# Layer 2 of a two-layer graph transformer: gathers two chunks ahead, four chunks of raw rows, ten of thirteen blocks of normalised rows turned inside rounds 0 and 1

## The chip, the core and the metric

The kernel runs on one core of one Trainium2 chip. The time is device microseconds of one execution, with all inputs and the output in the chip's memory; lower is better. Three runs of the kernel before gave 2701.38, 2709.74 and 2716.52 us, so the median is 2709.74 us.

The core has five engines, each with an instruction queue of its own that runs in order: TensorE (PE; PEld is its weight load), VectorE (DVE), ScalarE (ACT), GpSimd (POOL) and SyncE (SP). In this kernel SP issues most plain transfers, ACT issues a few, and POOL issues only the gathers of rows by index. Engines wait for each other, and for transfers, on semaphores.

## The reference

6250 nodes with 128 features and 106250 directed edges, sorted by target node. Two graph attention layers of 2 heads with 64 channels each; a batch norm and a ReLU between them; at the end a residual and a layer norm.

```python
def _transformer_conv(h, edge_attr, src, dst, Wq, bq, Wk, bk, Wv, bv, We, Ws, bs):
    q = (h @ Wq + bq).reshape(n, H, C)
    k = (h @ Wk + bk).reshape(n, H, C)
    v = (h @ Wv + bv).reshape(n, H, C)
    e = (edge_attr @ We).reshape(-1, H, C)
    alpha = jnp.einsum('ehc,ehc->eh', q[dst], k[src] + e) / jnp.sqrt(jnp.asarray(C, h.dtype))
    ex = jnp.exp(alpha - segment_max(alpha, dst)[dst])
    a = ex / segment_sum(ex, dst)[dst]
    out = segment_sum((v[src] + e) * a[:, :, None], dst)
    return out.reshape(n, H * C) + h @ Ws + bs

edge_attr = jnp.concatenate([cos((node_vec[src] - edge_weight) * time_w + time_b), msg], axis=-1)
h = _transformer_conv(x, edge_attr, ...layer 1)
h = relu((h - h.mean(0)) / jnp.sqrt(h.var(0) + 1e-05) * bn_g + bn_b)
x = _layernorm(x + _transformer_conv(h, edge_attr, ...layer 2))
```

## The kernel before

**Tiling.** The sorted edges are cut into NC = 106 chunks. A chunk has CE = 1024 edge slots (T = 8 tiles of 128) and NN = 64 target nodes, so 64 nodes times 2 heads fill the 128 partitions. All data is float32. The function `conv(c, extra, first_blocks)` (from L699) is called once for each layer, with c = 0 and c = 1. Everything is issued in an order written out by hand (`tc.manual_schedule()`), so the order of the Python calls is the order of each engine's queue.

**A round.** The loop at L934 has one round for each k. In round k of layer 2 PE does, in this order: `score(k, 0)` (L822 and L823: scores of 512 slots against the 128 node-and-head columns), `turn_weights(k-1)` (L845: 8 transposes of the exponentials), `score(k, 1)`, `finish_turn(k-2)` (L875, L876), `turn_in(k+1, 0)` and `turn_in(k+1, 1)` (L801: 4 transposes each of the gathered rows, tiles 0 to 3 and 4 to 7), some side work that `pull` takes from a generator (L627 and L1082: the score tables and the residual for later nodes), `finish(k-2)` (L897, L898), and `gather_sums(k-1)` (L853: 8 products that sum the rows by target node). DVE takes the lowest score (L828), divides by the softmax sum (L860 to L863, of k-2), copies the turned sums `fat` (L878, which L897 waits for) and copies the stored time encoding into the chunk (L982). ACT copies turned rows (L805, or L803 with batch norm and ReLU), turned weights (L846), and takes the exponential (L835).

**What a chunk needs from memory.** `fetch(k)` lets SP issue five loads in layer 2: the edge features (L726, 256 KB), the score table (L737, 128 KB), the time encoding `fz` (L740, 128 KB), the turned edge features `et` (L742, 448 KB) and the residual (L744, 32 KB). `gather(k, rows)` (L749) lets POOL fetch the 128 source rows of each of the 8 tiles, 64 KB each. Fetch and gathers run AHEAD = 4 chunks before use. From the second on, a gather in round k is tied to a step of PE in that round (`behind`): row 1 to `score(k, 0)`, row 2 to `turn_weights(k-1)`, row 3 to `score(k, 1)`, rows 4 and 5 to the two halves of `turn_in(k+1)`, and rows 6 and 7 to the second and the sixth product of `gather_sums(k-1)`.

**Buffers.** The chunk tile `ff` has AHEAD + 2 = 6 buffers, `fz` has 4, the residual 7, `et` 6. So in round k the tile of chunk k+4 takes the buffer of chunk k-2, whose last reader is `gather_sums(k-2)` in round k-1; and `fz` of chunk k+4 takes the buffer of `fz` of chunk k, which L982 reads late in round k. SP's queue stands at L740 until then.

**Between the layers.** Layer 1 leaves its result turned in SBUF (`hT`), and its rows unnormalised in memory (`h_d`). The batch norm's scale and shift are known once the last rows are there. Then `relu` (L1096) normalises `hT` block by block (13 blocks of 512 nodes), and `first_blocks` (L1098), called in the first round of layer 2, turns all 13 blocks back into rows and stores them to `hn_d`: for each block 4 transposes on PE (L1017), a copy on DVE (L1019, tile `fhr`, 3 buffers), and a store on SP (L1027, L1032). Chunks 0 to RAW - 1 = 2 do not wait for that: they gather raw rows from `h_d`, apply scale, shift and ReLU in the copy of the turned rows (L803), and normalise the rows themselves on DVE before they are summed (`normalise`, L868 and L869). From chunk 3 on rows come from `hn_d`; in the before kernel these gathers stand in round -1.

**Stores.** From round 11 of layer 2 on each round stores the output of one finished chunk: ACT scales it (`fout`, L923) and SP issues the store (L925), after SP's loads of that round.

Of the kernel before, what the change touches and what calls it, by code (L numbers as in the profile page):

```python
# [7 lines left out]
F32 = mybir.dt.float32  # L8
# [5 lines left out]
P = 128  # L14
D = 128
# [7 lines left out]
GE = GT * P  # L23
# [598 lines left out]
def tables(nc, pl, c, fT, b0, work, bank):  # L622

    o = work.tile([P, GE, H, 3 - c], F32, name="fo", tag="fo", bufs=1)
    for i, (a, b) in enumerate(pl.mats[c]):
        pg = bank()
        nc.tensor.matmul(pg, a, fT, start=True, stop=True)  # L627
        if i == 2 * H:
            nc.scalar.activation(o[:, :, :, 2], pg[:, :, None].to_broadcast([P, GE, H]), AF.Identity, bias=b)
        elif i < H:  # L630
            nc.scalar.activation(o[:, :, i, 0], pg, AF.Identity, bias=b)
        else:
            nc.vector.scalar_tensor_tensor(
                o[:, :, i - H, 1].rearrange("p (b n) -> p b n", n=P), pg.rearrange("p (b n) -> p b n", n=P), b,
                pl.code[:, None, :].to_broadcast([P, GE // P, P]), op0=OP.add, op1=OP.add)
# [25 lines left out]
def ordered(ctx: ExitStack, tc: tile.TileContext, pl, x, dst, edge_attr_64, conv2, bn_g, bn_b, out):  # L661
# [32 lines left out]

    SINGLE = 40

    RAW = 3

    def conv(c, extra, first_blocks=None):  # L699


        cs = ExitStack()
        load = cs.enter_context(tc.tile_pool(name=f"fload{c}", bufs=AHEAD + 2))
        work = cs.enter_context(tc.tile_pool(name=f"fwork{c}", bufs=2))
        small = cs.enter_context(tc.tile_pool(name=f"fsmall{c}", bufs=3))
        lnp = cs.enter_context(tc.tile_pool(name="fln", bufs=2)) if c else None
# [13 lines left out]
        def fetch(k):  # L720
            s = ch[k] = Plan()
            lo, hi = first(k)
            s.nb = nc.sync.value_load(pl.nbs[0:1, k:k + 1], min_val=lo, max_val=hi)
            sl = nc.sync.value_load(pl.sls[0:1, k:k + 1], min_val=0, max_val=E - CE)
            s.f = f = load.tile([P, T, FW], F32, name="ff")
            nc.sync.dma_start(f[:, :, 1 + D + TD:D + EW],  # L726
                              edge_attr_64[bass.ds(sl, CE), :].rearrange("(t p) d -> p t d", p=P))
            if c:
                nc.vector.memset(f[:, :, D + EW:1 + D + EW], 1.0)
            else:  # L730
                bits = small.tile([P, T, BITS], I32, name="fbits")
                nc.vector.tensor_tensor(bits, pl.dsts[:, :, k:k + 1].to_broadcast([P, T, BITS]),
                                        pl.bitm[:, None, :].to_broadcast([P, T, BITS]), OP.bitwise_and)
                nc.vector.tensor_scalar(f[:, :, D + EW:D + EW + BITS], bits, 0.0, None, op0=OP.is_equal)
                nc.vector.tensor_copy(f[:, :, D + EW + BITS:], bits)
            s.tab = load.tile([P, NN * H, 3 - c], F32, name="ftab")
            nc.sync.dma_start(s.tab, pl.tab_d[c][:, bass.ds(s.nb, NN)].rearrange("p n h w -> p (n h) w"))  # L737
            if c:
                s.z = load.tile([P, T, TD], F32, name="fz", bufs=AHEAD)
                nc.sync.dma_start(s.z, enc_d[k].rearrange("p (t d) -> p t d", d=TD))  # L740
                s.et = ets[k % len(ets)]
                nc.sync.dma_start(s.et, et_d[k])  # L742
                s.r = load.tile([NN, D], F32, name="fr", bufs=AHEAD + 3)
                nc.sync.dma_start(s.r, res_d[bass.ds(s.nb, NN), :])  # L744

        def gather(k, rows, behind=None):
# [7 lines left out]
                    behind = None  # L754

        shape = [P, T, TD]

        args, turned = [], []

# [56 lines left out]
        def score(k, u):  # L816

            s = ch[k]
            if u == 0:
                s.ps = p_s.tile([P, CE], F32, name="fps")  # L820
            w = slice(u * GE, (u + 1) * GE)
            nc.tensor.matmul(s.ps[:, w], s.tab[:, :, 0], s.ft[:, w], start=True, stop=False)  # L822
            return nc.tensor.matmul(s.ps[:, w], s.tab[:EC, :, 1], s.et[:, w], start=False, stop=True)  # L823
# [107 lines left out]
                next(gen, None)  # L931

        with cs, tc.manual_schedule():
            for k in range(-AHEAD, NC + 3):  # L934
                def on(j):
                    return 0 <= j < NC

                if on(k + AHEAD):
                    fetch(k + AHEAD)
                    gather(k + AHEAD, range(1))  # L940
                if k == -AHEAD and c:
                    first_blocks()
# [17 lines left out]
                if on(k + AHEAD):  # L960
                    gather(k + AHEAD, (4,), step)
                if on(k):
                    weigh(k)
                step = turn_in(k + 1, 1) if on(k + 1) else None
                if on(k + AHEAD):
                    gather(k + AHEAD, (5,), step)
# [12 lines left out]
                if c and on(k):  # L979
                    if k < RAW:  # L980
                        normalise(k)
                    nc.vector.tensor_copy(ch[k].f[:, :, 1 + D:1 + D + TD], ch[k].z)  # L982
# [3 lines left out]
                if on(k + AHEAD):  # L986
                    for t, step in zip((6, 7), steps):
                        gather(k + AHEAD, (t,), step)
# [9 lines left out]
    with tc.tile_pool(name="fpw", bufs=2) as pw:  # L998
# [3 lines left out]
        def pass_rows(b0):  # L1002

            r0 = b0 * GE
            n = min(GE, N - r0)
            rows = turned_rows(b0)
            nc.vector.bn_stats(stats[:, b0], hT[:, r0:r0 + n])
            yield
            put_rows(h_d, b0, rows)
            yield  # L1010

        def turned_rows(b0):
            r0 = b0 * GE
            n = -(-min(GE, N - r0) // P)
            pt = pl.bank().rearrange("p (b d) -> p b d", d=P)
            for i in range(n):
                nc.tensor.transpose(pt[:, i], hT[:, r0 + i * P:r0 + (i + 1) * P], ident)  # L1017
            rows = pw.tile([P, GE // P, P], F32, name="fhr", bufs=3)
            nc.vector.tensor_copy(rows[:, :n], pt[:, :n])  # L1019
            return rows  # L1020

        def put_rows(to, b0, rows):
            r0 = b0 * GE
            n = min(GE, N - r0)
            full = n // P
            if full:
                nc.sync.dma_start(to[r0:r0 + full * P, :].rearrange("(b p) d -> p b d", p=P), rows[:, :full])  # L1027

            left = n - full * P
            for a, b in ((0, left // 16 * 16), (left // 16 * 16, left)):  # L1030
                if a < b:
                    nc.sync.dma_start(to[r0 + full * P + a:r0 + full * P + b, :], rows[a:b, full])  # L1032

        def rest():
            def second():
# [304 lines left out]
```

## Time and profile before

| what | us |
|---|---|
| median of the three runs | 2709.74 |
| the profiled execution: its own time | 2705.18 |
| its span, first to last instruction | 2703.3 |
| granted TensorE clock, mean over the span | 0.947 |
| PE busy | 2331.9 |
| POOL busy (its gathers from `xv_d` 819.0, from `hn_d` 781.5) | 1628.4 |
| DVE busy / ACT busy | 1238.1 / 1234.0 |
| first `relu` block, after layer 1 has ended | 1371.62 |
| first gather of layer 2 | 1372.52 |
| first `turn_in` of layer 2 (chunk 0) | 1412.58 |
| start of round 3 of layer 2 | 1461.51 |
| last gather | 2645.20 |

The profile is of one execution. "Busy" is time in which an engine executes; the idle time of an engine that nobody waits for costs nothing. The chain of waits follows the work that ended last back from instruction to instruction, and tells at each step what released it. "Issue" is time in which an engine waited for nothing that the profile shows, and "remote", or "another core or an unknown queue", is a release whose sender the profile can't name. The times in a list of instructions are from the span's start.

### The profile page before, as it was taken

Reading aid. Unit: us, or ns where it says so; the run is one execution under the profiler, and the core shown is the slowest. Engines: PE = TensorE matmul, PEld = TensorE weight load, DVE = VectorE, ACT = ScalarE, POOL = GpSimd, SP = SyncE. Lnnn points to the kernel's source line nnn. Section 1 sums busy time; section 2 is a strip of 40 time slices with the busy share of each in tenths; the row PEclk is TensorE's granted clock in tenths of the full one; section 3 lists DMA queues with packets and bytes.
Section 4 is the critical chain, followed back from the end, with each engine's and each line's share of the span. In section 5 each row is a group of like instructions: output and inputs, shape, how many; then the busy total and the mean of one; then the engine's idle time right before and its main releaser. Section 6 shows DMA issues by size and latency. Waiting matters only on the chain. (4 is left out here: it accounts for less than half of the span.)

```text
span 2703.3 us, 40520 instructions
## 1 busy us (share of the span) xinstructions
PE 2331.9 (86%) x11586; PEld 1763.4 (65%) x11586; DVE 1238.1 (46%) x3738; ACT 1234.0 (46%) x1955; POOL 1628.4 (60%) x1717
## 2 busy tenths in 40 slices
PE   5799889998898998898957888898888889888887
PEld 3577667777776776776735666666666666666665
DVE  4466556666565665666533333333333333333223
ACT  2566666665555554545523333343333333333344
POOL 4666666666666666666336666666666666666660
PEclk7899999999999999999978999999999989999999
DMA  6555555555555455555447555565555555545441
GB/s 207 140 160 153 142 150 160 152 131 157 154 158 160 127 164 164 139 149 147 112 117 189 161 143 151 143 159 153 153 154 143 152 150 152 153 134 139 130 130 37
DMA packets 431127, 396.68 MB, mean 147 GB/s; under 512 B 279697, under 2 KB 375182, under 8 KB 427566
## 3 DMA queue, kind: packets, MB, share of 16 engines
q1 hardware_dynamic: 357680, 239.73, 31.9%
q0 software_dynamic: 54656, 113.07, 17.4%
q10 hardware_dynamic: 18558, 41.20, 4.3%
q8 instruction: 95, 1.56, 0.2%
q14 instruction: 138, 1.13, 0.1%
HBM read 277.19 MB, written 113.17 MB: 144 GB/s over the span
## 5 line engine op out<-in xcount | busy, mean ns | idle before, releaser
L749 POOL DMA_INDIRECT ff<-xv_d,fsrcs x848 | 819.0, 966 | 489.4 <-issue 169.6
L749 POOL DMA_INDIRECT ff<-hn_d,fsrcs x824 | 781.5, 948 | 462.4 <-issue 173.8
L853 PE MATMUL fpa<-ff,fpt 128*128 128x225 f32 x3392 | 754.2, 378 | 3.3 <-issue 2.7
L853 PEld LDWEIGHTS fpa<-ff,fpt 128*128 128x128 f32 x3392 | 675.9, 205 | 29.0 <-issue 6.2
L805 ACT COPY fft<-fpx 128x512 f32<-128x512 f32 x418 | 244.5, 585 | 579.2 <-PE fpa L853 164.6
L822 PE MATMUL fps<-fft,ftab 128*128 128x512 f32 x848 | 451.5, 614 | 45.4 <-ACT fs L835 24.4
L846 ACT COPY fpt<-fppt 128x512 f32<-128x512 f32 x424 | 234.7, 587 | 511.2 <-PE fppt L845 172.7
L878 DVE COPY fat<-fpo 128x256 f32<-128x256 f32 x212 | 90.0, 425 | 641.9 <-PE fpx L801 180.9
L845 PEld LDWEIGHTS fppt<-fident,fs 128*128 128x128 f32 x1696 | 199.5, 141 | 110.7 <-issue 106.7
L828 DVE TENSOR_REDUCE flow<-fps 128x1 f32<-128x1024 f32 x212 | 257.5, 1215 | 16.2 <-PE fpg L627 10.8
L835 ACT ACTIVATE fs<-fps,fm 128x1024 f32<-128x1024 f32 x212 | 236.8, 1117 | 34.0 <-DVE fm L830 14.6
L801 PE MATMUL fpx<-fident,ff 128*128 128x128 f32 x1696 | 240.5, 275 | 8.5 <-issue 7.2
L823 PE MATMUL fps<-fet,ftab 112*128 112x512 f32 x424 | 219.0, 597 | 8.7 <-issue 8.7
L845 PE MATMUL fppt<-fident,fs 128*128 128x128 f32 x1696 | 222.4, 273 | 3.5 <-issue 1.7
L823 PE MATMUL fps<-fxT,ftab 112*128 112x512 f32 x424 | 220.0, 600 | 2.8 <-issue 2.8
L822 PEld LDWEIGHTS fps<-fft,ftab 128*128 128x128 f32 x848 | 165.0, 227 | 64.9 <-ACT fs L835 37.1
L801 PEld LDWEIGHTS fpx<-fident,ff 128*128 128x128 f32 x1696 | 196.3, 142 | 15.3 <-issue 13.2
L823 PEld LDWEIGHTS fps<-fet,ftab 112*128 112x128 f32 x424 | 106.4, 251 | 85.7 <-issue 80.1
L897 PE MATMUL fpo<-fwv,fat 128*64 128x64 f32 x424 | 64.5, 246 | 110.7 <-issue 104.9
L811 ACT COPY fet<-fpe 112x512 f32<-112x512 f32 x212 | 126.5, 597 | 73.1 <-PE fpa L853 35.3
L823 PEld LDWEIGHTS fps<-fxT,ftab 112*128 112x128 f32 x424 | 84.4, 200 | 103.7 <-issue 103.0
L897 PEld LDWEIGHTS fpo<-fwv,fat 128*64 128x64 f32 x424 | 44.2, 146 | 158.9 <-issue 143.1
(202 smaller groups left out, 2438.1 us busy)
## 6 DMA issues: line engine op xcount, KB each, us to landing
ff<-in_edge_attr SPq DMA_DIRECT2D x212, 256.0 KB
et_d<-fet SPq DMA_DIRECT2D x106, 448.0 KB
fxT<-et_d SPq DMA_DIRECT2D x106, 448.0 KB
ftab<-tab_d SPq DMA_DIRECT2D x106, 192.0 KB
tab_d<-fo ACTq DMA_DIRECT2D x13, 1536.0 KB
ff<-xv_d,fsrcs POOLq DMA_INDIRECT x848
enc_d<-fzs SPq DMA_DIRECT2D x106, 128.0 KB
ftab<-tab_d SPq DMA_DIRECT2D x106, 128.0 KB
```

Source lines behind the costliest of these rows:

```text
L749: row = nc.gpsimd.indirect_dma_start(out=f[:, t, (1 if c else 0):1 + D], out_offset=None, in_=(h_d if k < RAW else hn_d) if c else pl.xv_d ...
L801: last = nc.tensor.transpose(px[:, t * P:(t + 1) * P], s.f[:, u * 4 + t, 1:1 + D], ident)
L805: nc.scalar.copy(s.ft[:, u * GE:(u + 1) * GE], px)
L811: nc.scalar.copy(s.et[:, u * GE:(u + 1) * GE], pe[:EC])
L822: nc.tensor.matmul(s.ps[:, w], s.tab[:, :, 0], s.ft[:, w], start=True, stop=False)
L823: return nc.tensor.matmul(s.ps[:, w], s.tab[:EC, :, 1], s.et[:, w], start=False, stop=True)
L828: nc.vector.tensor_reduce(low, s.ps, AX.X, OP.min)
L835: nc.scalar.activation(s.s, s.ps, AF.Exp, bias=s.bias, scale=-1.0)
L845: last = nc.tensor.transpose(pp[:, t * P:(t + 1) * P], s.s[:, at:at + P], ident)
L846: nc.scalar.copy(s.pt[:, u * GE:(u + 1) * GE], pp)
L853: nc.tensor.matmul(s.pa, s.pt[:, t * P:(t + 1) * P], s.f[:, t, 1:1 + D + EW], start=t == 0, stop=t == T - 1)
L897: nc.tensor.matmul(po[:NN, 0, r], at[:, 0, :, h], wv[c][:, r], start=True, stop=False)
```

## The change

Layer 1 keeps its order. In layer 2:

- `lead(k)` is 2: the loop starts at k = -2, and in round k the loads and gathers of chunk k+2 are issued instead of those of chunk k+4. The ties of each gather to a step of PE stay as they are. `ff`, the tables and `et` have 5 or 6 buffers (5 for the pool, `et` 6), `fz` 4, the residual 6.
- In the first round the first five gathers of chunk 0 are issued at once, and the other three are tied to the last product of the first table block (`pl.step`).
- `first_blocks` now only does the 12 remaining `relu` blocks. The 13 blocks of normalised rows are turned by `hide(n)`: one after each of the first three PE steps of round -1, five in round 0 and five in round 1, where they take the place of the `pull` of side work. The copies go to a tile of their own (`fhn`, 4 buffers). The first block of side work is so pulled from round 2 on.
- RAW is 4: chunk 3 gathers raw rows as well, and chunk 4, in round 2, is the first that reads `hn_d`.
- The flag `filling` is always False.

```diff
@@ tables @@
-        nc.tensor.matmul(pg, a, fT, start=True, stop=True)
+        pl.step = nc.tensor.matmul(pg, a, fT, start=True, stop=True)
...
-    RAW = 3
+    RAW = 4
+
+    hidden = list(range(-(-N // GE)))
...
-        load = cs.enter_context(tc.tile_pool(name=f"fload{c}", bufs=AHEAD + 2))
+        load = cs.enter_context(tc.tile_pool(name=f"fload{c}", bufs=5 if c else AHEAD + 2))
...
-                s.r = load.tile([NN, D], F32, name="fr", bufs=AHEAD + 3)
+                s.r = load.tile([NN, D], F32, name="fr", bufs=6)
...
+        def lead(k):
+            return 2 if c else AHEAD
+
+        def yield_first(bring):
+            if not c:
+                bring(range(T))
+                return
+            bring(range(5))
+            bring(range(5, T), pl.step)
+            first_blocks()
+
+        def hide(n):
+            step = None
+            for b0 in hidden[:n]:
+                step = put_rows(hn_d, b0, *turned_rows(b0, small.tile([P, GE // P, P], F32, name="fhn", bufs=4)))
+            del hidden[:n]
+            return step
...
-            for k in range(-AHEAD, NC + 3):
+            for k in range(-lead(-NC), NC + 3):
                 def on(j):
                     return 0 <= j < NC
 
-                if on(k + AHEAD):
-                    fetch(k + AHEAD)
-                    gather(k + AHEAD, range(1))
-                if k == -AHEAD and c:
-                    first_blocks()
-                step = score(k, 0) if on(k) else None
-                if on(k + AHEAD):
-                    gather(k + AHEAD, (1,), step)
-                step = turn_weights(k - 1) if on(k - 1) else None
-                if on(k + AHEAD):
-                    gather(k + AHEAD, (2,), step)
+                coming = [j for j in range(k + lead(k - 1), k + lead(k) + 1) if on(j)]
+                filling = False
+
+                def bring(rows, behind=None):
+                    for j in coming:
+                        gather(j, rows, behind)
+
+                for j in coming:
+                    fetch(j)
+                if k == -lead(-NC):
+                    yield_first(bring)
+                elif k < -1:
+                    bring(range(T))
+                elif not filling:
+                    bring(range(1))
+                step = score(k, 0) if on(k) else hide(1) if c and k == -1 else None
+                if k >= -1 and not filling:
+                    bring((1,), step)
+                step = turn_weights(k - 1) if on(k - 1) else hide(1) if c and k == -1 else None
+                if k >= -1 and not filling:
+                    bring((2,), step)
                 place()
                 if on(k - 2):
                     divide(k - 2)
-                step = score(k, 1) if on(k) else None
-                if on(k + AHEAD):
-                    gather(k + AHEAD, (3,), step)
+                step = score(k, 1) if on(k) else hide(1) if c and k == -1 else None
+                if k >= -1 and not filling:
+                    bring((3,), step)
...
                 if k >= 0:
                     at_round[0] = k
-                    pull(extra, 2 if k < 4 or k > 96 else 1)
+                    if c and k < 2:
+                        hide(5)
+                    else:
+                        pull(extra, 2 if k < 4 or k > 96 else 1)
...
@@ turned_rows, put_rows: return the last transpose; rows may be given @@
...
@@ first_blocks @@
             for b0 in range(1, NT):
                 relu(b0)
-            for b0 in range(-(-N // GE)):
-                put_rows(hn_d, b0, turned_rows(b0))
```

More of the change, by code (lines that the diff above doesn't have):

```diff
@@ L959, in conv @@
                 step = turn_in(k + 1, 0) if on(k + 1) else None
-                if on(k + AHEAD):
-                    gather(k + AHEAD, (4,), step)
+                if k >= -1:
+                    bring(range(5) if filling else (4,), step)
                 if on(k):
@@ L964, in conv @@
                 step = turn_in(k + 1, 1) if on(k + 1) else None
-                if on(k + AHEAD):
-                    gather(k + AHEAD, (5,), step)
+                if k >= -1:
+                    bring((5,), step)
                 for j in (k + 2,) if k < SINGLE else (k + 2, k + 3) if k == SINGLE else (k + 3,):
@@ L985, in conv @@
                 steps = gather_sums(k - 1) if on(k - 1) else (None, None)
-                if on(k + AHEAD):
+                if k >= -1:
                     for t, step in zip((6, 7), steps):
-                        gather(k + AHEAD, (t,), step)
+                        bring((t,), step)
             at_round[0] = 2 * NC
@@ L1008, in pass_rows, with turned_rows @@
             yield
-            put_rows(h_d, b0, rows)
+            put_rows(h_d, b0, *rows)
             yield
-        def turned_rows(b0):
+        def turned_rows(b0, rows=None):
             r0 = b0 * GE
@@ L1016, in turned_rows, with put_rows @@
             for i in range(n):
-                nc.tensor.transpose(pt[:, i], hT[:, r0 + i * P:r0 + (i + 1) * P], ident)
-            rows = pw.tile([P, GE // P, P], F32, name="fhr", bufs=3)
+                step = nc.tensor.transpose(pt[:, i], hT[:, r0 + i * P:r0 + (i + 1) * P], ident)
+            if rows is None:
+                rows = pw.tile([P, GE // P, P], F32, name="fhr", bufs=3)
             nc.vector.tensor_copy(rows[:, :n], pt[:, :n])
-            return rows
-        def put_rows(to, b0, rows):
+            return rows, step
+        def put_rows(to, b0, rows, step):
             r0 = b0 * GE
@@ L1032, in put_rows @@
                     nc.sync.dma_start(to[r0 + full * P + a:r0 + full * P + b, :], rows[a:b, full])
+            return step
         def rest():
```

## The prediction

> **What bounds the kernel now.** I read first the page's totals and slices, then the chain of waits between the layers, then the lists of instructions there, and last the rounds of layer 2.
>
> ```profile
> span 2703.3 us, 40520 instructions
> PE 2331.9 (86%) x11586; PEld 1763.4 (65%) x11586; DVE 1238.1 (46%) x3738; ACT 1234.0 (46%) x1955; POOL 1628.4 (60%) x1717
> ...
> PE   5799889998898998898957888898888889888887
> ...
> PEclk7899999999999999999978999999999989999999
> ```
>
> PE sets the time nearly everywhere, but slices 21 and 22 (1352 to 1487 us) fall to 5 and 7 tenths, with the granted clock down too: the passage between the layers. The chain of waits there:
>
> ```profile
> 1381.83 0.43 DVE fspread L1117
> 1382.25 3.56 another core or an unknown queue
> 1385.94 5.50 another core or an unknown queue
> 1391.53 6.21 another core or an unknown queue
> 1397.83 7.61 another core or an unknown queue
> ...
> 1422.17 5.39 issue
> ...
> 1431.08 11.77 another core or an unknown queue
> ```
>
> The columns are start, length, and what the chain stood on. The first line is work, the others are waits. The four after it are DVE's copies of the normalised rows (L1019): PE had turned those blocks by 1384.3, yet the copies start at 1385.89, 1391.46, 1397.76 and 1405.46. They make 22.9 us of signals that come late; the last two, 17.2 us, fall in rounds 0 to 2. While they last POOL issues gathers one after the other:
>
> ```profile
> 1401.29 0.95 POOL L749 DMA_INDIRECT ff<-h_d,fsrcs  x1 [0.30 <-issue]
> 1417.77 0.94 POOL L749 DMA_INDIRECT ff<-hn_d,fsrcs  x1 [15.53 <-DMA hn_d<-fhr]
> ```
>
> POOL has done its 24 raw gathers, then stands 15.5 us until `hn_d` is stored; chunk 0 could have been scored long before, but the 13 blocks stand ahead of it in PE's queue.
>
> Rounds, from the starts of L822 after L853: rounds 4 to 99 or so (94 that start between 1480 and 2600 us) take 11.94 us on average, though a round with no wait takes 10.15 (9.3 without side work). The difference is mostly L897, which waits for the copy `fat`. What SP does in that time:
>
> ```profile
> SPq L740 <- DVE ff L982: 105.3, 24, 9.0
> SPq L740 <- DVE finv L860: 84.5, 11, 10.2
> SPq L740 <- DVE finv L861: 58.3, 9, 8.8
> ```
>
> 248 us in which SP's queue stands at the load of `fz` (name of the wait, total, count, longest). The 448 KB load of `et` (L742) comes just behind it. Its place in the round goes with the round's length: where it is issued 3 to 1 us ahead of a round the round takes 10.22 us on average (20 rounds), at 1.5 to 3.5 us into it 12.72 (31 rounds), at 5 to 7 us 14.83 (3). In the first 5 us after it PE's signal to `fat` comes some 2 us late, after 6 us hardly late.
>
> **The change, part by part.**
>
> *The passage.* Before: 89.9 us from the first `relu` (1371.62) to the start of round 3 (1461.51). After: chunk 0's gathers still start at 1372.5 and take 8 x 1.25 us, to 1382.5; the `relu` blocks still end at 1384.2, and the table that chunk 0 needs is still stored at 1379.53 and loaded at 1384.30, with `fz`, `et` and the residual behind it. The three blocks turned in round -1 (12 transposes, about 2 us) lie beside that. Those loads kept the transfers busy until about 1391, so I let round 0 start at 1391 instead of 1414.1. Rounds 0 to 2 took 47.4 us. In them four L627 (0.95 us each at full clock) leave, 3.8 us, and ten blocks come in: 40 transposes, 0.66 to 1.1 us for four, 6.6 to 11 us; I take 10.8, since the clock is half there. DVE's ten copies (0.69 us each) and SP's stores lie beside other work. A copy waits for the store four before it to land; behind it in DVE's queue stand `normalise` of the same round and the next round's division, and `gather_sums` waits for `normalise`, one round later. The new tie of chunk 0's gathers 5 to 7 to the last table product (PE is done with it at 1378.18) costs nothing: POOL gets to the sixth at 1378.78. Of the 17.2 us of late signals I let 4 go, about a quarter, since most gathers of chunks 1 to 3 are now tied to a step of PE and run less in one stretch. Round 3 then starts at 1391 + 47.4 - 3.8 + 10.8 - 4 = 1441.4: a gain of 20 us. Bounds: if all of the 17.2 goes, 37; if the 22.9 us of late signals come back on ACT's copies of chunk 0, a loss of 3. The stores of `hn_d` (3.2 MB) now run against the loads of chunks 1 to 3; chunk 4's gather in round 2 needs them landed, and the last four took 2.4 us from issue to the gather's release, so nothing waits if round 1 issues them.
>
> *Fourth raw chunk.* `normalise` is 2 x 1.224 + 0.693 us of DVE (3.1 us) in round 3, between `fres` and the next division, where DVE has over 4 us until L875 is due; the ReLU copy costs 0.78 instead of 0.59 us on ACT. Nothing on the path; if that cover were gone, 3 us. The gathers that overlapped the three L868 pairs took 1.26, 1.31 and 1.35 us instead of 0.95, the next ones 0.98: 0.4 us of POOL. [...]
>
> *Two ahead instead of four.* A gather of row 7 tied to `gather_sums` in round k must have landed at the second half of `turn_in` in round k+1, and no longer two rounds later. POOL lags: in the trace row 7 starts 2.6 us (median) before that point. From issue to the last packet of a gather I see 2.7 us (the one at 1401.29, no packet after 1404) to 4 us (the last one, 2645.20, packets until 2649). At 3.3 us, 57 of 94 rounds would stand, 70 us in all, but in the same rounds PE stands afterwards anyway for L897; what goes beyond that is 20 us at 3.3, 38 at 4.0, 92 at 5.0. PE's standing also lets POOL catch up, and row 0 no longer waits for `gather_sums`, which alone cuts the 20 to 5. I take 10, between these two. The Trainium skill (DMA: Bandwidth & Descriptors, Anatomy of one DMA) has about 2.0 us plus bytes over 436 GB/s: an estimate of 2.15 us for 64 KB, with POOL's 0.95 us 3.1 us; by it the sum would be some 5 us lower.
>
> *SP's queue.* `fz` of chunk k+2 takes the buffer of k-2, so the wait of 248 us goes; so do POOL's and SP's waits for `gather_sums(k-2)` at row 0 and L726. SP then stands at the output store instead (L925, behind `fout`), and the five loads go out together, about 1 MB. From `fout` to the store are 0.42 us, from there to L726 2.3 to 4.3, to `et` 1.6 more: `et` first comes about 3 us into the next round, the long kind; but lateness there delays `fout`, and so the next `et`, towards 5 to 8 us. Late rounds: (20 x 10.22 + 3 x 14.83) / 23 = 10.82; early: 12.72. With half of each 11.77, that is 0.17 us less than now, over some 92 rounds 16 us. Bounds: all early, 92 x 0.78 = +72; all late, 92 x 1.12 = -103.
>
> *The end.* Gathers go on for two more rounds (to round 103). Rounds after the last gather take 9.3 us, those with gathers 11.94: +5.3.
>
> *Sum.* 2705.2 (the profiled execution) - 20 + 0 + 10 - 16 + 5.3 = 2684.5. The median of the runs shown stands 4.6 above that execution; I add half of it: **2687 us**.
>
> **The rivals.** (1) *SP's burst locks early* (slower): the 1 MB leaves 1 to 3 us into every round and each `fat` is late. For it: the 31 rounds at 12.72; against: each late round pushes the next burst later. 2687 + 16 + 72 = 2775; it decides once over about a fifth more of the rounds than half are of the early kind. (2) *Row 7 becomes the wait* (slower): if a gather lands 5 us after issue, +92 - 10: 2769; it decides above about 4.3 us. For it: POOL's lag; against: 2.7 to 4 us seen. (3) *The burst locks late*: rounds of 10.82, 2687 + 16 - 103 = 2600. (4) *The passage gives nothing*: the ten blocks keep their late signals inside rounds 0 and 1, and the change only moves the stall: 2687 + 20 = 2707.
>
> **How the numbers follow.** Forecast (2650 to 2696) 0.36; (3) and values below 2650 0.17; (4) 0.13; (1) 0.19; (2) 0.15. A measurement of this kernel can tell about 0.5% (13.5 us), so faster is below 2696: 0.53; same 0.13; slower (above 2723) 0.34. Range 2600 to 2778 leaves out some 0.1 at each side; the likeliest case alone spans 2650 to 2696.
>
> **What would show it.** Right: the first `turn_in` of layer 2 near 1385 and round 3 near 1441; POOL's 15.5 us gap gone; no wait of L740 on L982; L801's second half waiting for gathers under 0.3 us a round; mean round of 11.4 to 11.8. Wrong: L801 waiting for `ff` by 1 us or more in most rounds (2); L897 at 7.5 us or later in nearly all rounds with L742 at 1.5 to 3.5 (1); DVE's copies of `fhn` several us apart with PE behind them (4); rounds below 11 us (3).

## The result: 2688.4 us, and on other chips slower

The changed kernel took 2688.4 us (median of 6 runs, 2681.65 to 2690.39) where the kernel before took 2705.8 us (6 runs, 2700.78 to 2716.52): ratio 0.9928, 95% interval 0.9909 to 0.9948. The forecast was 2687 us. The agreement says less than it seems to: terms of the sum were wrong in opposite directions, and on two other chips used later the same change is a loss (ratio 1.0080, interval 1.0066 to 1.0094, and 1.0062, interval 1.0048 to 1.0076). Four chips come up below: A, that of the prediction's profile and of this first result; B, where the kernel before takes 2737 us; C and D, where it takes 2292 us. B, C and D were seen at one time each, so that a state of the machine at that time can't be told from a property of the chip. The sections below first read the changed kernel's profile on A. Its execution is the second fastest of the six (2681.86 us), while that of the kernel before (2705.18 us) lies at the median, so that the two profiles differ by 23.2 us and the medians by 17.4.

The page of the changed kernel on A: span, busy times, then the slices of PE and of its granted clock.

```profile
span 2680.1 us, 40399 instructions
...
PE 2333.5 (87%) x11586; PEld 1754.9 (65%) x11586; DVE 1242.1 (46%) x3741; ACT 1234.7 (46%) x1955; POOL 1623.1 (61%) x1717
...
PE   5799999998999898898968998989898888988886
...
PEclk7799999999999999999989999999999999999989
```

Of the two weak slices between the layers one is left, and the clock there falls to 8 tenths in one slice only. The rest of layer 2 looks as before. Cut at the first `relu` and at the start of round 4 of layer 2 it divides so: layer 1 was 2.7 us quicker in this execution (nothing there was changed), the passage takes 74.4 instead of 101.8 us (27.4 less), and from round 4 to the end it takes 1236.7 instead of 1229.9 us (6.8 more). The granted clock over the passage went up with it, from 0.77 to 0.87.

The chain of waits in the passage of the changed kernel (start, length, what it stood on):

```profile
1379.83 3.31 DMA ff<-h_d,fsrcs
1383.13 0.29 issue
1383.43 0.97 PE fpx L821
1384.40 0.03 issue
1384.42 0.78 ACT fft L823
1385.20 13.49 another core or an unknown queue
```

Chunk 0's rows are turned at 1381 to 1383.8, with no block ahead of them but the three of round -1; the last row had been asked for at 1379.83 and released PE 3.6 us later. Then ACT stands 13.5 us for the first half of chunk 1's turned rows. PE had turned it by 1392.25 (six transposes from 1391.43 on, 0.82 us), so that some 6.4 us of the wait are a late signal that has stayed. POOL issued 14 gathers without a pause from 1377.3 to 1394.5, and ACT went on at 1398.69, in the second of POOL's first two pauses (1394.5 to 1396.0 and 1397.0 to 1398.9).

DVE in rounds 0 and 1 (start, length, line, operation, tiles, and in brackets the idle time before it and its releaser), and POOL at chunk 4:

```profile
1407.01 0.69 DVE L1053 COPY fhn<-fpg 128x512 f32<-128x512 f32 x1 [4.81 <-DMA hn_d<-fhn]
...
1418.96 0.29 DVE L1053 COPY fhn<-fpg 128x128 f32<-128x128 f32 x1 [4.12 <-DMA hn_d<-fhn]
```

```profile
1422.61 0.98 POOL L751 DMA_INDIRECT ff<-hn_d,fsrcs  x1 [5.15 <-DMA hn_d<-fhn]
```

The copies do wait for the store four before theirs, with `normalise` behind them, so the last store is issued at 1419.28, in round 2, and chunk 4's first gather, which reads all of `hn_d`, waits 5.15 us. POOL's gap of 15.5 us has become one of 5.

Last the waits of rounds 4 and later (from 1480 to 2600 us; total, count, longest). First PE before the change, then PE and SP after it ("SPq" is SP's queue of transfers):

```profile
PE fpo L897 <- issue: 96.2, 46, 4.5
```

```profile
PE fpo L917 <- issue: 41.6, 28, 3.0
PE fpx L821 <- DMA ff<-hn_d,fsrcs: 31.3, 32, 4.7
PE fpx L821 <- issue: 17.2, 17, 2.9
```

```profile
SPq L945 <- ACT fpt L866: 99.0, 13, 22.9
SPq L945 <- ACT fout L943: 86.4, 23, 9.1
...
SPq L742 <- DVE flow L848: 0.8, 3, 0.4
```

L917 is the old L897, L821 the old L801, L945 the old L925, L742 the old L740. 54.6 us of waits for `fat` have gone and 48.5 us of waits for the last gathered rows have come; all waits of PE add up to 135 us before and 133 after. SP no longer stands at `fz`; it stands at the output store, as forecast. The mean round is 11.97 us (11.92 before, counted in the same way): nothing gained. The 6.8 us more lie at the end: rounds 4 to 99 take 1147.1 us instead of 1146.2, and from round 100 on it is 89.6 instead of 83.7.

### The profile page after: what moved, and what is told of

Same layout as the page of the kernel before. It is cut to its first block, busy times and chain, and to the rows that moved or that the text cites. A ratio compares the mean times of both kernels' runs of the same rounds, so it can differ in the third digit from the quotient of the medians.

```text
span 2680.1 us, 40399 instructions
## 1 busy us (share of the span) xinstructions
PE 2333.5 (87%) x11586; PEld 1754.9 (65%) x11586; DVE 1242.1 (46%) x3741; ACT 1234.7 (46%) x1955; POOL 1623.1 (61%) x1717
## 4 chain that ended last, share of the span: by engine, by line
PE 52%; issue 7%; DMA 5%; ACT 2%; another core or an unknown queue 1%; DVE 1%; POOL 1%; POOLq 0%; ACTq 0%; SPq 0%; DVEq 0%
PE fpa L873 18%; PE fps L842 8%; PE fps L843 8%; PE fppt L865 5%; PE fpx L821 4%; DMA ff<-hn_d,fsrcs 4%; PE fpg L627 2%; PE fpo L917 2%; PE fpe L830 1%; PE fpo L918 1%; POOL ff L751 1%; ACT fs L855 1%; PE fpo L895 1%; PE fpo L896 0%
## 5 line engine op out<-in xcount | busy, mean ns | idle before, releaser
L751 POOL DMA_INDIRECT ff<-hn_d,fsrcs x816 | 771.2, 945 | 455.4 <-issue 176.8
L873 PE MATMUL fpa<-ff,fpt 128*128 128x225 f32 x3392 | 734.5, 371 | 0.8 <-issue 0.8
L873 PEld LDWEIGHTS fpa<-ff,fpt 128*128 128x128 f32 x3392 | 661.4, 200 | 21.7 <-issue 2.5
L898 DVE COPY fat<-fpo 128x256 f32<-128x256 f32 x212 | 89.9, 424 | 633.5 <-PE fpx L821 247.7
L821 PE MATMUL fpx<-fident,ff 128*128 128x128 f32 x1696 | 258.2, 278 | 65.5 <-DMA ff<-hn_d,fsrcs 35.9
L848 DVE TENSOR_REDUCE flow<-fps 128x1 f32<-128x1024 f32 x212 | 257.3, 1214 | 21.6 <-PE fpg L1050 13.5
L821 PEld LDWEIGHTS fpx<-fident,ff 128*128 128x128 f32 x1696 | 199.5, 142 | 88.3 <-DMA ff<-hn_d,fsrcs 49.2
L855 ACT ACTIVATE fs<-fps,fm 128x1024 f32<-128x1024 f32 x212 | 236.7, 1116 | 33.9 <-DVE fm L850 11.5
L830 PE MATMUL fpe<-fident,ff 128*112 128x128 f32 x848 | 131.4, 279 | 15.3 <-issue 11.8
L796 DVE SCALAR_TENSOR_TENSOR farg<-fturns,farg 128x256 f32<-128x256 f32 x318 | 135.5, 426 | 10.9
```

The source lines that it names most:

```text
L751: row = nc.gpsimd.indirect_dma_start(out=f[:, t, (1 if c else 0):1 + D], out_offset=None, in_=(h_d if k < RAW else hn_d) if c else pl.xv_d ...
L796: nc.vector.scalar_tensor_tensor(arg, turn, -part, arg, op0=OP.mult, op1=OP.add)
L821: last = nc.tensor.transpose(px[:, t * P:(t + 1) * P], s.f[:, u * 4 + t, 1:1 + D], ident)
L830: last = nc.tensor.transpose(pe[:EC, t * P:(t + 1) * P], s.f[:, u * 4 + t, 1 + D:], ident)
L848: nc.vector.tensor_reduce(low, s.ps, AX.X, OP.min)
L855: nc.scalar.activation(s.s, s.ps, AF.Exp, bias=s.bias, scale=-1.0)
```

## The experiments

Each kernel's time is set against runs of the kernel before on the same chip. "Passage" is always the time from the first `relu` to the start of round 4, "rest" from there to the end of the span; they come from the one profiled execution of each. The unedited kernels were not profiled on B, nor the kernel before on C. In e4_no_et and e9_plain a part of the computation is left out.

| kernel | chip | median us | ratio to before (95%) | passage | rest |
|---|---|---|---|---|---|
| before | A | 2705.8 | | 101.8 | 1229.9 |
| after | A | 2688.4 | 0.9928 (0.9909 to 0.9948) | 74.4 | 1236.7 |
| e1_front | B | 2719.3 | 0.9944 (0.9923 to 0.9965) | 77.5 | 1251.5 |
| e3_before_fz5 | B | 2737.0 | 1.0003 (0.9988 to 1.0018) | 100.3 | 1244.6 |
| e4_no_et | B | 2718.7 | 0.9939 (0.9919 to 0.9960) | 73.8 | 1249.3 |
| e5_lead3 | B | 2723.2 | 0.9946 (0.9929 to 0.9964) | 74.0 | 1255.8 |
| a_after | C | 2309.0 | 1.0080 (1.0066 to 1.0094) | 71.5 | 1049.4 |
| e7_seven | C | 2302.3 | 1.0056 (1.0042 to 1.0070) | 67.5 | 1045.2 |
| e8_before_hold | C | 2301.4 | 1.0051 (1.0038 to 1.0065) | 76.5 | 1039.8 |
| e9_plain | C | 2281.0 | 0.9956 (0.9940 to 0.9971) | 68.9 | 1025.4 |
| b_before | D | 2287.8 (one run) | | 71.0 | 1032.6 |
| e8b_hold | D | 2305.7 (one run) | | 78.4 | 1040.1 |
| a2_after | D | 2306.3 | 1.0062 (1.0048 to 1.0076) | 71.1 | 1052.5 |
| e10_three | D | 2292.1 | 1.0001 (0.9992 to 1.0010) | 74.2 | 1033.5 |

**Which part of the change pays for the passage.** The blocks go back in front of chunk 0, all else stays:

```diff
-    hidden = list(range(-(-N // GE)))
+    hidden = []
...
-                    if c and k < 2:
-                        hide(5)
-                    else:
+                    if True:
...
+            for b0 in range(-(-N // GE)):
+                put_rows(hn_d, b0, *turned_rows(b0))
```

> The changed kernel (2688 us) with one part undone: all 13 blocks of normalised rows are turned ahead of chunk 0, as before; the lead of two chunks and four raw chunks stay. Theory A (the blocks in TensorE's queue are what the passage paid for): the gain goes, the first relu to the start of round 3 takes 85 to 92 us (before 89.9, after 61.4), total 2712 to 2718 us. Theory B (the signals were late because of 24 to 32 raw gathers issued in one stretch, and the shorter lead cures that wherever the blocks stand): round 0 starts some 9 us later than in the changed kernel, rounds 0 to 2 get the ten blocks back, first relu to round 3 takes 58 to 68 us, total 2685 to 2695 us. Both parts needed: in between, about 2700.

The passage took 77.5 us, and 67.3 to the start of round 3: theory B's range of 58 to 68, though the total of 2719 is to be read by its ratio, 0.9944, since chip B is slower all through. DVE's copies of the blocks, once the first stores have landed:

```profile
1414.82 1.36 DVE L1051 COPY fhr<-fpg 128x512 f32<-128x512 f32 x2 [5.88 <-DMA hn_d<-fhr]
1416.69 0.69 DVE L1051 COPY fhr<-fpg 128x512 f32<-128x512 f32 x1 [0.51 <-DMA hn_d<-fhr]
1417.99 0.69 DVE L1051 COPY fhr<-fpg 128x512 f32<-128x512 f32 x1 [0.61 <-DMA hn_d<-fhr]
```

There is one long wait for a buffer (5.88), and then a copy every 0.9 to 1.3 us; the four waits for late signals are gone although the 13 blocks stand where they stood before. From the first `relu` to chunk 0's scores it is 28.9 us instead of 42.5. So the shorter lead with its fourth raw chunk carries 23 to 24 of the passage's 27 us (101.8 or 100.3 to 77.5), and the hiding of the ten blocks some 3 to 4 us (77.5 to 73.8 and 74.0 in e4_no_et and e5_lead3, the two kernels on the same chip that have the changed passage). Of that, 1.7 us are only moved: two rounds' worth of side work that e1_front does before round 4 and those two after it. In the whole time no gain of the hiding is seen: the ratios are 0.9944 without it, and 0.9939 and 0.9946 with it. That the number of gathers in one stretch is the cause (12 in one stretch beside the blocks' copies instead of 24) fits, but the lead and the raw chunks were changed together with it.

**SP's wait at `fz` by itself**, in the kernel before:

```diff
-                s.z = load.tile([P, T, TD], F32, name="fz", bufs=AHEAD)
+                s.z = load.tile([P, T, TD], F32, name="fz", bufs=AHEAD + 1)
```

> The kernel before (2706 us) with a fifth buffer for fz and nothing else, so that SP no longer stands at the load of fz (L740, 248 us over the run): the prediction's step on SP's queue alone, with the lead still four chunks. The prediction's step: rounds of layer 2 fall from 11.94 to about 11.77, 16 us less, 2690 us; with its bounds 2603 to 2778, decided by when the load of et is issued in the round. Rival (where et is issued goes with the round's length without being its cause): the wait at L740 goes, the issue of et moves, the mean round stays within 11.85 to 12.0 and the time within 2700 to 2712 us.

SP's and PE's waits in the rounds of layer 2 (1500 to 2620 us):

```profile
SPq L925 <- ACT fpt L846: 169.4, 25, 9.3
SPq L925 <- ACT fout L923: 88.0, 18, 12.2
```

```profile
PE fpo L897 <- issue: 101.2, 48, 4.8
```

The wait at L740 is gone, the wait for `fat` is what it was, and the time is the same within 0.2%. The table of `et`'s place in the round, on which the prediction built 16 us, has turned over: rounds with `et` issued 3.5 to 7 us into them take some 11 us here (30 to 41 rounds, by how a load is assigned to a round) and took 13.8 to 14.8 before (11 rounds); in the changed kernel rounds with `et` 3 to 1 us ahead of them take 13.3 us (22 rounds), before 10.2 (20). Place and length went together, but the place did not make the length.

**The load of `et` taken away** in the changed kernel:

```diff
-                nc.sync.dma_start(s.et, et_d[k])
+                if k < len(ets):
+                    nc.sync.dma_start(s.et, et_d[k])
```

> The changed kernel without the 448 KB load of et from chunk 6 on (the scores of chunks 6 to 103 of layer 2 are made with old rows: that part of the computation is left out, all instructions on PE, DVE, ACT and POOL stay). If et's burst is what makes TensorE's signals late (the prediction's reading of the phase table), rounds fall from 12.0 to 10.3 to 10.8 and the total to 2530 to 2580 us. If the row gathers (512 KB in each round) or POOL make them late, and et is only one load more, rounds stay at 11.5 or above and the total at 2640 us or above. If no transfer has to do with it, 2680 to 2695.

```profile
PE fpo L918 <- issue: 55.2, 33, 4.7
PE fpx L822 <- DMA ff<-hn_d,fsrcs: 29.0, 36, 2.1
```

PE's waits (1500 to 2620 us) stay. Rounds take 12.1 us, and the rest 1249.3 us, against 1251.5 in e1_front, which has all loads and the same lead. 46 MB of transfers fewer make a difference of some 2 us between two executions: the bursts of `et` are not what the rounds wait for. By the ranges written down this is "11.5 or above", but the ratio, 0.9939, is also that of the third case, "no transfer has to do with it" (2680 to 2695 of 2706 us): the run rules out `et` and does not tell the gathers from the rest.

**A lead of three chunks from round 6 on:**

```diff
-            return 2 if c else AHEAD
+            return (2 if k < 6 else 3) if c else AHEAD
```

> The changed kernel with layer 2 gathering three chunks ahead from round 6 on (the passage is untouched; fz has four buffers, so SP does not stand at it either). The waits of PE for the last row of the next chunk (L821, 31 us for the transfer and 17 us more, 49 times) must go. If they are a cost of their own, as the prediction's second rival has it, the time falls by 30 to 48 us, to 2640 to 2660. By the prediction's step (they stand in the place of waits for fat that come anyway, 10 us net) it falls by about 10, to 2678. If the waits only change places, 2684 to 2692, with the waits of L917 back at 80 to 96 us (42 now, 96 before).

```profile
PE fpo L917 <- issue: 82.9, 44, 5.7
PE fpo L917 <- DVE fat L898: 13.3, 6, 5.5
```

PE's waits again from 1500 to 2620 us: no wait for gathered rows is left, and the waits for `fat` are back at 83 us (49.4 in e1_front on the same chip). The ratio, 0.9946, is that of e1_front. The waits only change places here, as far as this shows: the one round in which two chunks are gathered, 16 gathers, took 20.8 us, some 10 us that the other two kernels on B don't pay, so that a gain of a few us may be hidden.

**The changed kernel on another chip,** unedited:

> The changed kernel unedited, on the chip of this call, so that the others can be set against it. Ratio to the kernel before 0.991 to 0.995 again; first relu to the start of round 3 some 61 us (61.4, 59.7 and 62.8 in the three runs so far that have its passage), round mean in layer 2 within 0.1 us of the kernel before.

The ratio is 1.0080: slower by 17 us, which neither the prediction's sum nor the expectation had. The clock granted is 0.985 (0.953 on A), and a round that waits for nothing takes the same 9.3 or 10.1 us as on A, but here 77 of the 96 rounds 4 to 99 are of that kind (27 on A). The passage to round 3 is 54.8 us instead of some 61. To see what the kernel before does on such a chip it was profiled on D, where the changed kernel ran too:

> The kernel before, unedited, for its trace on the chip of this call. On a chip on which it takes some 2290 us (no signal late there): by the difference of the runs of that chip the passage (first relu to round 3) is 55 to 59 us, 2 us more than the 54.8 of the changed kernel, waits of PE for gathered rows 8 to 14 us after round 2 (25.5 there), rounds of 10.0 us; that is what makes the changed kernel 17 us slower there. If the passage were still near 66 us (as in the kernel that held chunk 1 back), the loss of the changed kernel would have to lie in its rounds with more than 25 us. On a chip on which it takes some 2700 us: as in the trace shown, 90 us and 11.9 us.

> The changed kernel, unedited, beside the others of this call. If the kernel before takes some 2700 us on this chip, ratio 0.991 to 0.996; if it takes some 2290 us, ratio 1.006 to 1.010 again. If the ratio does not go with the kind of chip, the reading that the gain consists of late signals falls.

The kernel before on D, its page and PE's waits from 1250 to 2270 us; then the changed kernel on D, the same two views:

```profile
span 2285.9 us, 40520 instructions
...
PE 2205.7 (96%) x11586; PEld 1703.8 (75%) x11586; DVE 1234.3 (54%) x3738; ACT 1227.4 (54%) x1955; POOL 1626.0 (71%) x1717
...
PE   5999999999999999999978999999999999999997
```

```profile
PE fpx L801 <- DMA ff<-hn_d,fsrcs: 8.7, 18, 0.9
```

```profile
span 2305.8 us, 40399 instructions
...
PE 2209.9 (96%) x11586; PEld 1708.5 (74%) x11586; DVE 1239.8 (54%) x3741; ACT 1231.3 (53%) x1955; POOL 1629.9 (71%) x1717
```

```profile
PE fpx L821 <- DMA ff<-hn_d,fsrcs: 22.7, 20, 2.1
```

No wait of L897 or L917 put down to "issue" is left, where A and B have 42 to 101 us: the late signals are not seen in these rounds. Nor are they seen in the passage. DVE's copies before the change, on D, wait for buffers, once for 5.68 us and then for at most 1.3, with POOL in the middle of its 24 gathers:

```profile
1201.69 2.17 DVE L1019 COPY fhr<-fpg 128x512 f32<-128x512 f32 x3 [5.68 <-DMA hn_d<-fhr]
```

The passage takes 71.0 and 71.1 us: what the change gains up to round 3 (54.8 against 60.9 us, where 55 to 59 had been expected) it gives back in round 3, which takes 16.3 us instead of 10.1. All of the loss, 19.9 us, lies in the rest: 14.0 in waits for gathered rows (22.7 against 8.7), 1.7 in two more rounds with other work in them (56 against 54, 0.87 us each; the blocks' products that rounds 0 and 1 no longer do come later), and 4 that the lists of waits do not name. These go with the clock: in rounds 4 to 99 the changed kernel has three stretches of 3.4 us at half clock, which cost up to 5 us, and the kernel before has none. Round 3's loss on C, in the chain of waits of a_after:

```profile
1238.31 0.98 POOL ff L751
1239.29 0.30 issue
1239.60 7.82 DMA ff<-hn_d,fsrcs
1247.46 0.47 PE fpx L821
```

That is chunk 4: its gathers began at 1230.69, after 4.1 us of POOL's waiting for the last store of `hn_d`, and the last row, asked for at 1239.60, came 7.8 us later. PE stood 3.4 us in all for the last two rows, and the side work behind them (four L627, two in the kernel before) took 3.4 us at a granted clock of 0.54; at full clock four take 1.9. In the 7.8 us the core's 16 DMA engines were busy all the time (224 GB/s; in the rest of this execution a share of 0.63 and 167 GB/s), so the row probably stood behind other transfers. The Trainium skill (DMA: Bandwidth & Descriptors, Anatomy of one DMA) gives 2.0 us and the bytes over 436 GB/s, an estimate of 2.15 us for such a row; the 3.3 us seen above on A includes POOL's 0.94 and comes near it, the 7.8 us do not.

**Chunk 1's gathers held back** in the kernel before, so that 8 gathers instead of 24 run beside the blocks (two runs, as C had no late signal to take away, and neither had D):

```diff
-                    gather(k + AHEAD, range(1))
+                    gather(k + AHEAD, range(1), pl.turned if c and k == 1 - AHEAD else None)
...
-                nc.tensor.transpose(pt[:, i], hT[:, r0 + i * P:r0 + (i + 1) * P], ident)
+                pl.turned = nc.tensor.transpose(pt[:, i], hT[:, r0 + i * P:r0 + (i + 1) * P], ident)
```

> The kernel before with one dependency more: the first gather of chunk 1 waits for the last transpose of the 13 blocks, so that POOL issues 8 gathers instead of 24 while DVE copies those blocks; lead, raw chunks and the place of the blocks stay. Theory B (a long stretch of gathers makes the signals between the engines late): the copies follow each other in 1 to 2.5 us instead of 5.5 to 7.6, relu to the first turn of chunk 0's rows takes 27 to 33 us instead of 41.9, and part of it is lost again as chunks 1 and 2 come later; relu to round 3 in 70 to 85 us (89.9 before), time 5 to 20 us below the kernel before. If the copies are late for another reason (the wait for stores, the clock), they stay 5 to 8 us apart, and the time is 0 to 10 us above the kernel before, since chunk 1 comes later.

> The kernel before with the first gather of chunk 1 held until the 13 blocks are turned, once more, since the chip of the last call had no late signals to take away. On a chip on which the kernel before takes some 2700 us, theory B (a long stretch of gathers makes signals late): copies 1 to 2.5 us apart, relu to the first turn of chunk 0's rows 27 to 33 us, relu to round 3 70 to 85 us (89.9). If the stretch is not the cause: copies still 5 us or more apart, 85 to 100 us. On a chip of some 2290 us: 28 and 66 us again.

Chunk 0's scores begin 28.0 and 27.5 us after the first `relu`, against 29.4 in the kernel before on D: the copies are no quicker without the gathers, since they were not late. The passage is 5.5 and 7.4 us longer than that of the kernel before on D, as chunk 1 comes later. Whether a long stretch of gathers makes the signals late on chips like A and B could be settled by this kernel only there, and there it was not run.

**Seven buffers for the turned rows** in the changed kernel:

```diff
-                step = put_rows(hn_d, b0, *turned_rows(b0, small.tile([P, GE // P, P], F32, name="fhn", bufs=4)))
+                step = put_rows(hn_d, b0, *turned_rows(b0, small.tile([P, GE // P, P], F32, name="fhn", bufs=4) if b0 % 7 < 4 else None))
```

> The changed kernel with seven buffers for the turned rows instead of four (the three idle fhr buffers are used in turn with fhn's four), so that no copy in rounds 0 and 1 waits for the store four before it (4.81 and 4.12 us on DVE in the changed kernel, normalise and the division of round 2 behind them). If those waits stand on the path, rounds 0 to 2 fall from 46.5 us to 40 to 43 and the time by 4 to 7 us (0.15 to 0.25%) against the changed kernel of the same call. If they lie beside the late signals of those rounds, round 3 starts within 2 us of where it did and the ratio is the same within 0.1%.

6.7 us below the changed kernel on the same chip, and the passage 4.0 us shorter (67.5 against 71.5). The two intervals just touch (1.0042 to 1.0070, 1.0066 to 1.0094), so the sign is likely and the size is not sharp; the waits probably stood on the path there.

**The gathers replaced** from chunk 12 on, in the changed kernel:

```diff
+            if c and k >= 12:
+                if 0 in rows:
+                    nc.sync.dma_start(f[:, :, 1:1 + D], hn_d[:CE, :].rearrange("(t p) d -> p t d", p=P))
+                return
```

> The changed kernel with the rows of layer 2 from chunk 12 on brought by one ordinary load of 1024 consecutive rows (the same 512 KB in 512-byte rows, issued by SP) instead of eight gathers by POOL; those chunks work on the wrong rows, so that part of the computation is left out. If POOL's gathers are what makes the signals of the rounds late, rounds fall from 12.0 to 10.2 to 10.8 and the time by 105 to 160 us. If the bytes that move count and not who asks for them, rounds stay at 11.5 to 12.0 and the time falls by less than 45 us. If neither, 11.9 to 12.1.

It ran on C, so it could not tell what makes signals late. It does tell what the gathers cost with a lead of two where no signal is late: the rest falls from 1049.4 to 1025.4 us, 7 us below even the kernel before on D. (The one load also asks for all rows at the start of a round, so that this is not POOL's share alone.) Eight gathers take POOL 8 x 1.25 = 10.0 us; a round takes PE 9.3 or 10.1. POOL can hardly catch up once it is behind.

**A version with three edits:** five raw chunks, seven buffers, a lead of three from round 1 on.

```diff
-    RAW = 4
+    RAW = 5
...
-            return 2 if c else AHEAD
+            return (2 if k < 1 else 3) if c else AHEAD
```

> The changed kernel with three edits: five raw chunks instead of four, seven buffers for the turned rows, and a lead of three chunks from round 1 on (the extra chunk's gathers then fall into rounds that are long anyway). If the row waits and the store behind chunk 4's gather are what the changed kernel loses, it gains 8 us by the buffers and the store, 10 to 13 by the row waits of layer 2 and 3 at the end: some 20 us below the changed kernel where the kernel before takes some 2290 us (ratio to before 0.998 to 1.002), and 5 to 10 us below it where it takes some 2700 us (ratio 0.988 to 0.993). If the eight gathers more in round 1 make PE wait for rows there, or signals late, it stands 0 to 10 us above the changed kernel.

```profile
PE fpx L821 <- DMA ff<-hn_d,fsrcs: 11.3, 13, 2.2
```

PE's waits from 1250 to 2270 us: those for rows are halved, and the rest is 1033.5 us, that of the kernel before (1032.6). It takes 14 us less than the changed kernel on D, and the same as the kernel before (1.0001, interval 0.9992 to 1.0010). What it pays is in the passage: the eight gathers more of round 1 are late for round 2, where PE waits for five rows, 7.5 us in all, for one of them 3.48, and round 2 is 21.7 us long (12.9 in the changed kernel):

```profile
1238.75 0.48 PE L821 MATMUL fpx<-fident,ff 128*128 128x128 f32 x1 [3.48 <-DMA ff<-h_d,fsrcs]
```

So it beats the changed kernel on D, and on C and D no version that computes the whole beats the kernel before. It was not run on a chip like A or B.

## Why the prediction was right, step by step

*The passage: right in direction, mis-sized, and for the lesser reason.* 20 us were forecast to the start of round 3 and 28.5 measured on A (89.9 to 61.4; to the start of round 4 it is 27.4). Chunk 0's scores began 14.9 us after the first `relu` instead of the 19.4 that the step had: it supposed that the loads keep the transfers busy until then, and the last row was there 14.5 us after it. Rounds 0 to 2 took 46.5 us, forecast 50.4. Of the late signals 4 us were let go "about a quarter"; by e1_front their going is most of the gain. The upper bound of 37 counts these 4 twice: 20 and the other 13.2 make 33.2. Three details were wrong. "Nothing waits if round 1 issues them": the last stores were issued in round 2, and POOL waited 5.15 us. The tie of gathers 5 to 7 "costs nothing": POOL stood 1.49 us ahead of the sixth gather, where 0.30 is usual. And the four L627, taken off as 3.8 us, are not gone: the same work stands in later rounds, so that this item moves the start of round 3 and does not belong in the sum.

*Fourth raw chunk: 0, not told apart.* It is inside the passage of e1_front.

*Two ahead: the gross cost about right, the net cost a matter of the chip.* 70 us of standing were forecast before the cover by L897, and 48.5 came. On A the cover is whole: PE's waits sum to the same. On B e5_lead3, which takes the waits for rows away, shows no gain. So the net there is nearer 0 than 10. On D, where no wait for `fat` covers anything, the rest is 19.9 us longer, the upper end of the step's 5 to 20, and e10_three with its lead of three gets it back.

*SP's queue: the step that failed.* -16 us were forecast, and e3_before_fz5 measured 0 (the interval reaches from 3 us less to 5 us more). The waits moved as the step said, from L740 to the output store, but its price came from a correlation. The rounds in which signals were late also shifted the load, since L740 waited for DVE's copy, which stands behind those signals; that this is why the two went together is argued, that the load does not make the length is shown by e3_before_fz5 and e4_no_et. The mean round of 11.4 to 11.8 us, named as a sign, did not appear.

*The end: +5.3, and +5.9 measured* from round 100 on, on A, in one execution of each kernel whose single rounds there vary from 9.3 to 16.2 us.

*The sum: luck.* The rest as a whole was forecast at 10 - 16 + 5.3 = -0.7 and is +6.8; the passage is 7.4 better than forecast. These two errors cancel. Two smaller ones do so too: layer 1, which nothing changed, was 2.7 us quicker in the profiled execution, and the median of the runs lies 6.5 us above that execution, where 2.3 had been added. So 2687 meets 2688.4.

*The rivals.* (2), row 7, comes on A as waits, but not as time; on C and D it is most of the loss, though a quarter of the size that the rival had. (4), a passage that gives nothing, is what D shows, 71.0 against 71.1 us, but not for its reason: no late signal is there to be moved, and the gain goes in round 3, half of it in waits for chunk 4's rows (3.0 of 6.2 us on D). (1) and (3) rested on the table of `et` and fall with it. None of the cases allowed that the stalls might come and go with the chip and not with the kernel, and this goes with the sign.

## What to carry to other kernels

A wait that the profile puts down to no producer in the program ("issue", "another core or an unknown queue") may be absent on another chip or at another time: before time is spent on it, profile the same kernel on a second chip, since a change that trades slack for such waits can gain 0.7% on one and lose 0.8% on the next. A table that sorts rounds by where something was issued gives a price only after an edit has moved that one thing alone; one buffer more was enough to show it. Work that leaves a passage is gained only if it vanishes, so look where its instructions stand afterwards.

## What the runs showed of the hardware

The same program, the kernel before, took 2706 and 2737 us on two chips and 2292 us on two others, with granted clocks of 0.947 (A's profile) and 0.935 to 0.945 (B) against 0.983 to 0.987 (C and D). By the sums the clock is the lesser part: PE was busy for 2332 us of 2703 on A and for 2206 us of 2286 on D, so that 126 us of the difference are slower work and 291 are idle time (371 against 80 us).

The two go together, though. In rounds 4 to 99 of the kernel before on A the profile has 26 stretches of 3.4 or 6.8 us at half clock, and in the 3.4 us ahead of each of them PE had been idle for 1.8 us or more (0.42 on average over these rounds). The 26 rounds with such a stretch take 14.6 us on average, the other 70 take 10.9; on D there is no such stretch in these rounds, and they take 9.9. So in these rounds on A a long wait was paid for twice, first as idle time and then as slow work.

What delays the signals on A and B remains open: it is not the 448 KB loads, and the gathers were only seen beside the longest delays. On C and D PE sets the pace of layer 2 (busy for 1007.5 of the 1032.6 us from round 4 on in the kernel before on D), with POOL close behind: a gather every 1.25 us, eight to a round of 10.1.
